# The order of two pairs of branch arms, with prefetch hints for the jumps over the arms not taken

## The chip, the core and the metric

The kernel runs on one core of a Trainium2 chip. A core has five engines that run side by side, each with its own stream of instructions and its own sequencer: TensorE (PE, matmuls; its weight loads are shown as PEld), VectorE (DVE), ScalarE (ACT), GpSimd (POOL) and SyncE (SP, which here only issues transfers). They meet through semaphores. Data moves between the chip's memory and the on-chip buffer by DMA, and so does code: the instructions lie in memory and are fetched in blocks.

The metric is the device time of one execution, in microseconds, as the median of several runs. A branch is taken by each engine for itself: all five load the flag into a register and jump or fall through, each at its own time.

## What is computed

One layer of a Perceiver-like network in float32, for 256 tokens of width 512: attention with 16 heads over 4096 context positions and the tokens themselves, then a state-space block (Mamba-2), then a mixture of 32 experts of which each token uses 6, with a shared expert beside them. Each part adds to the residual stream. Cut to what matters here:

```python
x = x + attention(layernorm(x), ctx, wq, wk, wv, wo, wk_ctx, wv_ctx, q_norm_w, k_norm_w)
x = x + mamba2(layernorm(x), W_in, conv_w, conv_b, dt_bias, A_log, D, norm_weight, W_out)

h = layernorm(x)
scores = sigmoid(h @ gate_w)
topk_w, topk_i = top_k(scores, 6)
topk_w = topk_w / (sum(topk_w) + 1e-20)
routed = sum over the 6 experts e of topk_w[e] * ((silu(h @ wg[e]) * (h @ wu[e])) @ wd[e])
shared = (silu(h @ sg) * (h @ su)) @ sd
return x + routed + shared
```

## The kernel before

The tokens stand in two tiles of 128 (`NT = 2`, `x_sb[:, t, :]`). Ahead of everything (L85 to L110) small constants are made, SP issues the first loads (the first piece of the context, `wk_ctx` in three pieces, `x`, the rest of the context's first piece, `wv_ctx`), and DVE works out a flag `small_scores` from the norm weights: whether attention scores are bounded so that the softmax needs no running maximum.

**The outer branch** (L1601, L1602). `values_load` lets every engine load the flag. The whole layer is then written twice, once as `layer(lctx, True)` (bounded scores) and once as `layer(lctx, False)` (the general case). In this program the arms lie in memory in the order in which the code has them: bounded, general, closing. With the inputs used here the flag is 1 and the bounded arm runs. Its first work on PE is the projection of the first context piece to keys (`ps_k`, L220), which waits for that piece and for `wk_ctx`.

**The inner branch** (L1558, L1572). The experts are computed in `NP = 16` rounds of two experts. The rounds have room for a certain number of tokens per expert; an expert with more is "crowded", and `crowded` says whether there is one. The value is loaded into `some` on every engine (L1558, in the middle of the rounds; each engine reaches the load where the order built for it puts it). At the end, if `some == 0`, the cheap arm runs: `finish(t)` adds the last sums, which PE has accumulated in `total[t]`, to `x_sb`, and `store(t)` sends the tile to the output, tile by tile. Otherwise the crowded arm computes all experts once more in full, and only then stores. With these inputs the cheap arm runs. In memory it lies between the rounds and the crowded arm, and behind that lies the whole general arm (on PE alone 3,823 instructions as the program is written, ahead of their expansion, and its own two inner arms), and then the closing code at L1651. So in the run shown every engine falls through both tests and then, at the end of the cheap arm, jumps over the crowded and the general arm to the closing code; the jump is on record under L1572 too.

At the end of an arm each engine raises the semaphores by what the other arm would have added, so that both arms leave the same counts. GpSimd does that for the counts of its indirect transfers with one instruction, `INC_SWDGE_SEM`.

**The closing code** (L1651). SP waits for all transfers and engines (12 semaphore instructions), then every engine passes a barrier: a DRAIN, then a semaphore that POOL gathers from the other four and releases. POOL clears the semaphores, and a second barrier follows.

What sets the order around the change: the scheduler places instructions by their dependencies within each engine's stream, block by block between branches. The order on SP is what matters for stores: an instruction waiting there holds up those behind it.

## Time and profile before

| | us |
|---|---|
| median of 3 runs | 983.04 (982.28 to 983.1) |
| the profiled execution | 983.11 |
| its span, first to last instruction | 981.4 |
| granted TensorE clock, mean | 0.997 of full |

Where the span goes, by stretches (busy time of PE in each):

| stretch, us | what runs | PE busy, us |
|---|---|---|
| 0 to 12 | constants, first loads, first keys | 6.8 |
| 12 to 730 | attention | 718 |
| 730 to 840 | state-space block, routing | 105 |
| 840 to 960 | rounds of experts | 120 |
| 960 to 972.8 | last round, last sums | 12 |
| 972.8 to 981.4 | stores, jump, closing code | 0 |

The page gives busy time per engine, but leaves out branches, semaphores, register loads and DMA issues. Those are found by asking for one line of the kernel: each row then names the engine (a "q" behind it is the engine's sequencer: "POOLq"), the operation, how often it stands there, its duration in ns (least, median, most) and when the first and the last of them started. "PEldq" is PE's sequencer. COMPARE_BRANCH is the record of any branch, conditional or not.

### The profile page before, as it was taken

The numbers are of one execution on the slowest core, as the hardware profiler recorded it, in microseconds if no ns is written. First come the engines' busy times: TensorE is split into PE (matmuls) and PEld (weight loads), VectorE is DVE, ScalarE is ACT, GpSimd is POOL, SyncE is SP. The second block draws the span as 40 slices with busy tenths as digits, with TensorE's granted clock in tenths as the row PEclk, the third lists the DMA queues.
The fourth block names the chain that finished last, engine by engine and source line by source line (L and its number), as shares of the span: only waits on it lengthen the run. The fifth ranks groups of instructions, "written<-read, shape, count | busy, mean of one in ns | idle before, by whom it ended". The sixth has DMA issues, their size and how long they took to land.

```text
span 981.4 us, 8877 instructions
## 1 busy us (share of the span) xinstructions
PE 961.9 (98%) x2730; PEld 454.0 (46%) x2730; DVE 497.0 (51%) x1000; ACT 388.0 (40%) x854; POOL 204.5 (21%) x212
## 2 busy tenths in 40 slices
PE   7999999999999999999999999999999999999996
PEld 3444444444444444444444444444465655555432
DVE  4456554454454544544545445358587656622124
ACT  3645443443443434434434344353153642122221
POOL 4443001101100200200200110000014133545433
PEclk9999999999999999999999999999999999999998
DMA  9734142213304304304213121160036353899974
GB/s 325 232 75 124 50 118 86 54 34 116 86 11 139 86 1 150 76 11 150 54 33 79 72 65 30 57 171 1 0 140 218 132 184 135 305 367 350 379 300 124
DMA packets 131164, 125.65 MB, mean 128 GB/s; under 512 B 80065, under 2 KB 99298, under 8 KB 125858
## 3 DMA queue, kind: packets, MB, share of 16 engines
q1 hardware_dynamic: 119216, 77.96, 26.5%
q0 software_dynamic: 7984, 41.16, 11.3%
q10 hardware_dynamic: 3906, 5.85, 1.7%
q8 instruction: 24, 0.39, 0.2%
q14 instruction: 34, 0.28, 0.1%
HBM read 89.02 MB, written 35.93 MB: 127 GB/s over the span
## 4 chain that ended last, share of the span: by engine, by line
PE 95%; ACT 1%; DVE 1%; POOL 1%; issue 0%; DMA 0%; SPq 0%; DVEq 0%
PE oT L594 23%; PE scT L569 23%; PE ps_kv L366 17%; PE ps_egu L220 5%; PE ps_self L220 3%; PE ps_v L220 2%; PE ps_o L792 2%; PE ps_egu L1390 2%; PE ps_k L220 2%; PE ps_ye L1460 2%; PE ps_xbc L220 1%; PE ps_out L986 1%; PE ps_sgu L220 1%; PE xgTp L1371 1%; PE ps_ye L1463 1%; PE ps_ye L1413 1%
## 5 line engine op out<-in xcount | busy, mean ns | idle before, releaser
L585 DVE TENSOR_TENSOR lacc<-lacc,prT 128x512 f32<-128x512 f32 x256 | 182.9, 715 | 239.0 <-ACT prT L575 238.3
L575 ACT ACTIVATE prT<-scT,bq,rk 128x512 f32<-128x512 f32 x256 | 198.8, 777 | 254.1 <-PE scT L569 241.7
L569 PE MATMUL scT<-qT,kT 128*128 128x512 f32 x536 | 271.6, 593 | 0.0
L594 PE MATMUL oT<-prT,v 128*128 128x512 f32 x528 | 268.3, 592 | 0.0
L569 PEld LDWEIGHTS scT<-qT,kT 128*128 128x128 f32 x536 | 101.2, 190 | 124.6 <-issue 121.4
L594 PEld LDWEIGHTS oT<-prT,v 128*128 128x128 f32 x528 | 100.3, 190 | 125.7 <-issue 115.5
L198 POOL TENSOR_TENSOR rk<-pv,mhalf 128x4 f32<-128x4 f32 x32 | 32.3, 1010 | 369.3 <-DVE pv L197 369.3
L256 ACT ACTIVATE sq<-kraw 128x128 f32<-128x128 f32 x128 | 35.6, 278 | 45.2 <-DVE kraw L384 43.2
L366 PE MATMUL ps_kv<-wkv,fast 128*128 128x512 f32 x112 | 53.5, 592 | 0.0
L366 PE MATMUL ps_kv<-wkv,ctx 128*128 128x512 f32 x112 | 52.8, 592 | 0.0
L366 PE MATMUL ps_kv<-fast,fast 128*128 128x512 f32 x112 | 52.6, 592 | 0.0
L600 DVE TENSOR_TENSOR oacc<-oT,oacc 128x512 f32<-128x512 f32 x64 | 43.7, 683 | 0.0
L366 PEld LDWEIGHTS ps_kv<-fast,fast 128*128 128x128 f32 x112 | 21.3, 190 | 26.8 <-issue 21.8
L366 PEld LDWEIGHTS ps_kv<-wkv,fast 128*128 128x128 f32 x112 | 21.3, 190 | 26.8 <-issue 26.8
L366 PEld LDWEIGHTS ps_kv<-wkv,ctx 128*128 128x128 f32 x112 | 21.3, 190 | 26.8 <-issue 23.7
L360 POOL TENSOR_TENSOR fast<-ctx 128x512 f32<-128x512 f32 x7 | 9.3, 1335 | 113.1 <-PE ps_kv L366 94.2
L384 DVE TENSOR_TENSOR kraw<-ps_kv,fast 128x256 f32<-128x256 f32 x42 | 17.8, 424 | 28.2 <-PE ps_kv L366 28.2
L1443 DVE TENSOR_TENSOR hid<-si,ps_egu 128x128 f32<-128x128 f32 x18 | 5.2, 286 | 49.8 <-ACT si L1441 49.8
L792 PE MATMUL ps_o<-wo,qT 128*128 128x512 f32 x64 | 28.8, 592 | 0.0
L220 PE MATMUL ps_self<-wq,xT 128*128 128x512 f32 x64 | 28.1, 592 | 0.0
L605 DVE RECIPROCAL lacc<-ps_l 128x512 f32<-128x512 f32 x8 | 26.8, 3348 | 0.1
L366 PE MATMUL ps_kv<-fast,ctx 128*128 128x512 f32 x56 | 26.3, 592 | 0.0
(379 smaller groups left out, 1118.8 us busy)
## 6 DMA issues: line engine op xcount, KB each, us to landing
xg<-xn SPq DMA_DIRECT2D x6, 2560.0 KB, 9.3
ctx<-in_ctxT_dram SPq DMA_DIRECT2D x7, 1024.0 KB, 5.3
kd<-tr SPq DMA_DIRECT2D x112, 64.0 KB, 2.4
kT<-kd SPq DMA_DIRECT2D x28, 256.0 KB, 2.9
ye<-y_sb ACTq DMA_DIRECT2D x21, 256.0 KB, 8.2
wq<-in_wq_dram SPq DMA_DIRECT2D x4, 1024.0 KB, 14.7
wo<-in_wo_dram SPq DMA_DIRECT2D x4, 1024.0 KB, 7.4
w_in<-in_W_inT_dram SPq DMA_DIRECT2D x4, 1024.0 KB, 5.7
```

The source lines that it names most:

```text
L198: return G.tensor_tensor(dst, v[:, :n], mhalf[:, :n], ALU.pow)
L220: TE.matmul(ps, lhs(k), rhs_of(k), start=(k == 0), stop=(k == KD - 1))
L256: S.activation(sq[:, h, :], raw[:, h, :], AF.Square, accum_out=ss[:, h:h + 1])
L366: TE.matmul(ps, lhs(k), rhs(k), start=(start and k == 0), stop=(k == 1), skip_group_check=True)
L569: scored.append(TE.matmul(sc, kT[:, g, i * P:(i + 1) * P], qT[:, t, heads4(g), :].rearrange("p h q -> p (h q)"), start=True, stop=True).ins)
L575: S.activation(pr, sc, AF.Exp, bias=shift, scale=SCALE if r is None else r[:, i, g:g + 1])
L585: V.tensor_tensor(la, la, pr, ALU.add)
L594: TE.matmul(outs[g, t], v[:, i, g * HD:(g + 1) * HD], pr, start=(n == 0), stop=last)
L600: V.tensor_tensor(ov, outs.pop((g, t)), ov, ALU.add)
L605: V.reciprocal(rl, ps)
L792: TE.matmul(m["ps_o", t], aT[:, t, h, :], wo[j][:, h % 4, :], start=(h == 0), stop=(h == NH - 1))
L1390: TE.matmul(ps[self.half(i)], xT[:, k, self.half(i)], w[i][:, k, :], start=(k == 0), stop=(k == KD - 1))
```

## The change

The arms change places. The general arm comes first in the outer branch, so the test is turned round (`flag == 0`) and the bounded arm is reached by a jump. Of the inner branch only the crowded arm is left, `finish` moves ahead of it and `store` behind it: both sums are made first, then a jump leads over the crowded arm, then both stores are issued. The bounded arm is now the last code ahead of the closing code. Two calls mark places for a prefetch hint, on all five engines: `"general"` ahead of the load of the flag, `"crowded"` behind the rounds. Each becomes one instruction per engine that names its branch as likely taken. In the built program they are the first instructions of their blocks: the first ones of the kernel's body, and the first ones of the arm.

```diff
@@ -1557,6 +1557,7 @@
                     weights_back()
                     some = nc.values_load(crowded, min_val=0, max_val=1)
                 (main.turn_hidden if wide else main.turn_hidden_halves)(n)
+            tc.mark_branch_hint_location("crowded", "LikelyTaken", mybir.ALL_ENGINES)
 
             spread_last(NP - 2, [0])
             main.down_here(NP - 1)
@@ -1569,13 +1570,10 @@
             def store(t):
                 nc.sync.dma_start(out[t * P:(t + 1) * P, :], x_sb[:, t, :])
 
-            with tc.If(some == 0) as arms:
-                for t in range(NT):
-                    finish(t)
-                    store(t)
-            with arms.Else():
-                for t in range(NT):
-                    finish(t)
+            for t in range(NT):
+                finish(t)
+
+            with tc.If(some == 1, label="crowded"):
                 main.weights = {}
                 for n in range(NP):
                     main.weights[n] = (held[2 * (n % 2)], held[2 * (n % 2) + 1], rests[n % 2])
@@ -1596,15 +1594,17 @@
                 V.tensor_copy(row2, row2f)
                 for t in range(NT):
                     add(gather(ye2, row2, t, [(main.e4, "xg")] * TOPK), t)
-                    store(t)
-
+            for t in range(NT):
+                store(t)
+
+    tc.mark_branch_hint_location("general", "LikelyTaken", mybir.ALL_ENGINES)
     flag = nc.values_load(small_scores, min_val=0, max_val=1)
-    with tc.If(flag == 1) as arms:
+    with tc.If(flag == 0, label="general") as arms:
+        with ExitStack() as lctx:
+            layer(lctx, False)
+    with arms.Else():
         with ExitStack() as lctx:
             layer(lctx, True)
-    with arms.Else():
-        with ExitStack() as lctx:
-            layer(lctx, False)
```

In the bounded arm, the instructions of every engine stand in the same order as before, but for the hint at its head and, on DVE, the two sums ahead of the load of `crowded` instead of behind the test. The first store waits, as the second does, for DVE's semaphore after it has been raised for the skipped arm.

## The prediction

> **What bounds the kernel now.** I read four views: the page (busy shares, queues, chain), then the chain of waits at both ends, then the branch lines and the closing line one by one, since the change is about branches and the page does not count them as work.

> ```profile
> span 981.4 us, 8877 instructions
> PE 961.9 (98%) x2730; PEld 454.0 (46%) x2730; DVE 497.0 (51%) x1000; ACT 388.0 (40%) x854; POOL 204.5 (21%) x212
> ...
> q8 instruction: 24, 0.39, 0.2%
> q14 instruction: 34, 0.28, 0.1%
> ```

> TensorE (PE) is busy for 98% of the span, so only what lies before its first and after its last matmul can be won, and whatever starts PE later is paid in full. The last two rows are queues that carry instructions: code is fetched by DMA, 0.39 MB in 24 packets (16 KB each) on one queue, 0.28 MB in 34 packets (8 KB each, a few tiny) on the other.

> The chain of waits at the two ends (start us, length us, what):

> ```profile
> 1.26 3.85 DMA wkv<-in_wk_ctx_dram
> 5.10 0.14 issue
> 5.24 13.00 PE ps_k L220 x24
> ...
> 969.40 2.67 PE total L1430 x6
> 972.07 0.02 issue
> 972.10 0.69 DVE x_sb L1567
> ```

> PE starts when the first piece of wk_ctx has landed, at 5.1. Its last matmul ends at 972.1, the last sum at 972.8. The span ends at 981.4: **8.6 us in which no engine computes.** What fills them stands in the rows of L1572 (the inner branch and the jump behind its arm) and L1651 (the closing of the kernel); columns: duration ns min/median/max, first and last start.

> ```profile
> L1572 ACTq COMPARE_BRANCH  x2: 34/36/38, 969.8 to 970.1; - x2
> L1572 DVEq COMPARE_BRANCH  x2: 51/53/55, 969.9 to 972.1; - x2
> L1572 PEldq COMPARE_BRANCH  x2: 63/2064/4064, 970.5 to 972.3; - x2
> L1572 POOLq INC_SWDGE_SEM  x1: 1767/1767/1767, 969.6 to 969.6; - x1
> ...
> L1572 POOLq COMPARE_BRANCH  x1: 41/41/41, 971.4 to 971.4; - x1
> ...
> L1572 SPq COMPARE_BRANCH  x1: 38/38/38, 973.6 to 973.6; - x1
> ```
> ```profile
> L1651 SPq EVENT_SEMAPHORE  x12: 27/28/28, 976.9 to 977.7; - x12
> ...
> L1651 POOLq DRAIN  x3: 40/107/6594, 973.9 to 981.1; - x3
> L1651 SPq DRAIN  x3: 7/7/130, 977.7 to 980.8; - x3
> L1651 ACTq DRAIN  x2: 8/44/81, 972.6 to 980.8; - x2
> L1651 PEldq DRAIN  x2: 8/40/73, 976.4 to 980.9; - x2
> L1651 DVEq DRAIN  x2: 10/34/57, 976.4 to 980.8; - x2
> ```

> Each engine meets L1572 twice: the test (falls through in this kernel) and the jump over the arms that were not taken. After the jump nothing runs for long: ACT 970.1 to 972.6 (2.5 us), POOL 971.4 to 973.9 (2.5), SP 973.6 to 976.9 (3.3, a semaphore wait may be in it), PE 972.3 to 976.4 (4.1, the 4064 ns of its row), DVE 972.1 to 976.4 (4.3). In the window from 970 to 982, instruction packets show on both queues. So **a taken jump to far code costs 2.5 to 4.3 us here**, while the tests that fell through cost 34 to 98 ns. What ends last is POOL: its first DRAIN starts at 973.9, takes 6.594 us and ends at 980.5, 1.1 us after SP's (979.4 by the trace). From there 0.8 us of barriers lead to 981.4.

> **The change, part by part**, against the profiled execution: 983.1 us, of which 981.4 are span and 1.7 lie outside it; the median of the runs is 983.04, 0.1 less.

> *The jump behind the arms goes (end).* The cheap arm now stands last, so its end runs straight into the closing code. On POOL, INC_SWDGE_SEM still starts at 969.6 (it waits for the last gather) and lasts 1.77; DRAIN then follows at 971.4 instead of 973.9: 2.5 us less. If it keeps its 6.6 us it ends at 978.0. Next in line is SP, below. The other three reach their DRAIN by 973 and wait.

> *Sums ahead of the branch, stores behind it.* DVE does both sums, then loads `crowded` (0.33 us, row of L1558), tests (0.05), jumps, and raises its semaphore for the skipped arm. By the built order both stores now wait for that raise. Load and test run beside the second sum (0.69 us), so if the jump is cheap the stores issue at about 972.9 and 973.4; today 972.0 and 972.8. The row of L1570 gives 3.8 us from issue to landing: 977.2. Queued behind the stores on SP are only the closing waits, mostly done by then (12 take 0.8 us today), so 0.3 us more: SP is through at 977.5, still 0.5 ahead of POOL. Cost nothing, covered by POOL's DRAIN; without that cover the delay of 0.6 counts in full.

> *Jumps over the crowded arm.* Five taken jumps are new. SP makes its own at about 846, POOL at 965, ACT at 970, PE at 970.5, with nothing behind them for microseconds; even at 4.1 us PE is through by 974.6. DVE's alone is exposed, at 972.5, since stores wait for it.

> *Jumps over the general arm (start).* Today PE tests at 3.5 and waits for its load until 5.1, a slack of 1.6 us. SP tests at 5.5; the first thing it then loads, wk, is wanted at 22.7 and lands 13.7 us after its issue at 5.6, 3.4 us in hand. ACT and DVE wait for loads too (tables, x). So PE decides.

> *Hints.* One per engine as first instruction of the kernel, one as first instruction of the arm: the built order has the second there, 960 us ahead of its branch, not where the code places it. No row shows a hint. From both sides: if it works, a jump costs about what a test does, 0.1 us, and the start loses nothing on PE; if it does nothing, PE's jump costs the row's 4.1 us: 3.5 + 4.1 = 7.6 instead of 5.2, 2.4 us lost. I take the hint as working, as it executes at 0.8, 2.7 us ahead of the branch, more than ACT's or POOL's whole jump, when no load is yet moving; that is a choice. Its instruction takes its turn ahead of SP's first load (SP's small instructions: 0.03 to 0.1 us), and 16 KB of code for PE beside the first loads may hold one piece of wk_ctx up by as much as the fetch, up to 1 us. Between 0 and 1 us I take **0.3**, nearer the low end, as the fetch comes first.

> [...]

> **Sum:** -2.5 (POOL) + 0.3 (start) = -2.2: 983.1 - 2.2 = 980.9, less the 0.1 to the median: **980.8 us**.

> **Cases.** Under 0.2% (2 us here) a difference does not count as a change; so faster is below 981.1, slower above 985.0.

> 1. *As above*, 980.8: 980.5 to 981.5 by the start's 0 to 1, and 980.1 to 981.9 with half the spread of the runs shown (982.3 to 983.1) on either side: 0.40. For it: POOL's jump is plainly in its rows and its DRAIN follows directly.
> 2. *POOL's DRAIN gets shorter too*, as it might end with something else that also moves. Then SP closes: 977.5 at the latest, 975.7 if the stores land 1.8 us sooner without instruction packets beside them; with the 0.8 the span ends at 978.3 to 976.5, -3.1 to -4.9, and +0.3: 978.4 to 980.2, middle 979.4: 0.20. Against it: nothing names what the DRAIN waits for.
> 3. *Given back.* Either the DRAIN ends at 980.5 whatever happens before it, or the outer hint comes too late for PE (+2.4 against -2.5). 982.8 to 983.8: 0.23. Against the first: all gathers have landed by 969.4 and the count is raised at 971.3, which leaves nothing for it to wait on.
> 4. *The hints do nothing*: the new jumps are paid where somebody waits. Start +2.4. At the end DVE's jump at 972.5 costs 4.3: the stores issue at 976.9 and 977.3, land by 981.1, SP closes at 981.4 instead of POOL at 980.5: +0.9. 983.0 + 3.3 = 986.3. It decides from the point where PE's jump costs over 1.6 us, and DVE's over about 0.6. For it: [...]the early place of the second hint: 0.17.

> Faster: 0.28 of case 1 and all of case 2, 0.48. Same: 0.12 of case 1 and case 3, 0.35. Slower: case 4, 0.17. The range 978.6 to 985.3 leaves out most of case 4 and the fastest end of case 2. Case 1's own is 980.1 to 981.9.

> **What would show it.** L1576 in place of L1572: POOL's INC_SWDGE_SEM at 969.6 and DRAIN right behind it, with its length (6.6, or case 2 or 3). PE's first ps_k at 5.2 to 5.6 rather than 7.6. The stores at 972.9 and 973.4 rather than 977. No instruction packets from 970 on, and five early ones near 1 us. If PE's row of the outer branch shows about 4 us, the forecast is wrong at the hint; if POOL's DRAIN still ends at 980.5, it is wrong at the DRAIN.

## The result, and the profile after

| | before | after |
|---|---|---|
| median of the runs, us | 983.28 (8 runs, 982.28 to 985.02) | 985.72 (8 runs, 985.35 to 988.44) |
| the profiled execution, us | 983.11 | 985.35 |
| its span, us | 981.4 | 983.6 |
| first ps_k product starts, us | 5.2 | 9.4 |
| last sum ends, us | 972.8 | 977.8 |
| last sum to the span's end, us | 8.6 | 5.8 |

The ratio of the times is 1.003, 95% interval 1.0021 to 1.004: **slower by 0.3%**, where 980.8 us were forecast. The end gave about what was forecast (2.8 us, for 2.5), and the start lost 5.0.

The page of the kernel after, and its chain of waits at both ends (start us, length us, what):

```profile
span 983.6 us, 8882 instructions
PE 962.8 (98%) x2730; PEld 454.0 (46%) x2730; DVE 499.8 (51%) x1000; ACT 388.0 (39%) x854; POOL 204.8 (21%) x212
...
q8 instruction: 25, 0.41, 0.2%
q14 instruction: 34, 0.28, 0.1%
```
```profile
1.35 3.72 DMA wkv<-in_wk_ctx_dram
5.07 4.32 issue
9.38 13.61 PE ps_k L220 x24
...
977.09 0.02 issue
977.11 0.69 DVE x_sb L1568
```

The work is the same: 2730 matmuls, and PE busy for 0.9 us more. The first data are there at 5.07 as before, but between data and first product stand 4.32 us of "issue" in place of 0.14: PE waited for nothing that is data. One more 16 KB packet of code came in on q8. The branch rows of the outer test say where PE stood (duration ns min/median/max, first and last start us). First PE's row in the kernel before, then all engines in the kernel after, then the hints:

```profile
L1602 PEldq COMPARE_BRANCH  x1: 98/98/98, 3.5 to 3.5; - x1
```
```profile
L1602 ACTq COMPARE_BRANCH  x1: 68/68/68, 3.6 to 3.6; - x1
L1602 POOLq COMPARE_BRANCH  x1: 64/64/64, 3.7 to 3.7; - x1
L1602 PEldq COMPARE_BRANCH  x1: 5424/5424/5424, 3.7 to 3.7; - x1
L1602 DVEq COMPARE_BRANCH  x1: 78/78/78, 3.7 to 3.7; - x1
L1602 SPq COMPARE_BRANCH  x1: 70/70/70, 5.8 to 5.8; - x1
```
```profile
L1651 ACTq BRANCH_PREFETCH_HINT  x2: 35/48/60, 0.8 to 9.8; - x2
...
L1651 PEldq BRANCH_PREFETCH_HINT  x2: 31/40/50, 0.9 to 9.2; - x2
```

PE's record holds the whole stand at the jump, 5.4 us. The other engines' records end at once; how long they stood is read from the next instruction, which is the second hint: ACT tests at 3.6 and goes on at 9.8. So every engine stood for 5.1 to 6.3 us here, although its hint had run at 0.8 to 0.9. By the trace no packet of code starts before 6.75 (PE's), 3.05 us *after* PE's branch. It ends at 7.8, and PE goes on at 9.1, 1.3 us later. In every jump of these runs for which PE had to wait for code it goes on 1.3 to 1.8 us after its packet has ended, so it is the packet that it stands for. In the old jump the packet started 1.7 us after the branch. In the stretch from 5 to 9 us the 16 DMA engines are full with the first loads (share 1.02 to 1.07); in the old jump's stretch, 970 to 976, the share was 0.01 to 0.56.

The end, by the rows of the inner branch and of the closing code:

```profile
L1576 POOLq INC_SWDGE_SEM  x1: 1780/1780/1780, 974.4 to 974.4; - x1
L1576 ACTq COMPARE_BRANCH  x1: 54/54/54, 974.8 to 974.8; - x1
...
L1576 PEldq COMPARE_BRANCH  x1: 359/359/359, 975.5 to 975.5; - x1
...
L1576 DVEq COMPARE_BRANCH  x1: 68/68/68, 977.5 to 977.5; - x1
```
```profile
L1651 POOLq DRAIN  x3: 40/109/6525, 976.3 to 983.4; - x3
L1651 SPq DRAIN  x3: 7/7/7, 981.3 to 983.1; - x3
```

POOL's DRAIN now starts right behind INC_SWDGE_SEM (974.4 + 1.8), before the last sum ends; before it stood 2.6 us behind it. It takes 6.5 us as before and still closes the span. PE's jump over the crowded arm is 0.36 us where the jump of before was 4.1.

### The profile page after: what moved, and what is told of

The parts are those of the page before. It is cut to its first block, busy times and chain, and to the rows that moved or that the text cites. A ratio compares the mean times of both kernels' runs of the same rounds, so it can differ in the third digit from the quotient of the medians.

```text
span 983.6 us, 8882 instructions
## 1 busy us (share of the span) xinstructions
PE 962.8 (98%) x2730; PEld 454.0 (46%) x2730; DVE 499.8 (51%) x1000; ACT 388.0 (39%) x854; POOL 204.8 (21%) x212
## 3 DMA queue, kind: packets, MB, share of 16 engines
q0 software_dynamic: 7984, 41.16, 11.4%
## 4 chain that ended last, share of the span: by engine, by line
PE 95%; ACT 1%; DVE 1%; issue 1%; POOL 1%; DMA 0%; SPq 0%; DVEq 0%
PE scT L569 23%; PE oT L594 23%; PE ps_kv L366 17%; PE ps_egu L220 5%; PE ps_self L220 3%; PE ps_v L220 2%; PE ps_o L792 2%; PE ps_egu L1390 2%; PE ps_k L220 2%; PE ps_ye L1460 2%; PE ps_xbc L220 1%; PE ps_out L986 1%; PE ps_sgu L220 1%; PE xgTp L1371 1%; PE ps_ye L1463 1%
## 5 line engine op out<-in xcount | busy, mean ns | idle before, releaser
L220 PE MATMUL ps_self<-wq,xT 128*128 128x512 f32 x64 | 28.1, 592 | 0.0
L220 PE MATMUL ps_k<-wkv,ctx 128*128 128x512 f32 x32 | 17.2, 700 | 9.4 <-issue 9.4
```

What stands on the lines that cost most here:

```text
L220: TE.matmul(ps, lhs(k), rhs_of(k), start=(k == 0), stop=(k == KD - 1))
```

## The experiments

The question was which part does what, and why one hint worked and the other did not. My theory at first, called **block theory** below: code is read in blocks (in the kernel before, PE's 16 KB packets come once per some 250 records of its stream), and a hint is acted on only if its branch stands in a block that is entered after the hint has run. The inner hint has 960 us and many blocks between it and its branch; the outer one has, on PE, only the load of the flag. The rivals: the lead of 2.7 us is too short (**lead theory**), or the loss has another cause. Below, "jump" is the time from the branch to the next instruction that the engine meets behind it.

### One part at a time

The outer edit undone (`e1_inner_only`), the inner edit undone (`e2_outer_only`), each hint taken out (`e3_no_outer_hint`, `e4_no_inner_hint`):

```diff
# e1: outer branch as before
-    with tc.If(flag == 0, label="general") as arms:
+    with tc.If(flag == 1) as arms:
# e2: inner branch as before
-            with tc.If(some == 1, label="crowded"):
+            with tc.If(some == 0) as arms:
# e3
-    tc.mark_branch_hint_location("general", "LikelyTaken", mybir.ALL_ENGINES)
# e4
-            tc.mark_branch_hint_location("crowded", "LikelyTaken", mybir.ALL_ENGINES)
```

> The inner branch as in the changed kernel, the outer branch in the old order: its bounded arm comes first again and there is no outer hint. Block theory (a hint is acted on only where an engine's program comes to the branch in a stretch of code that it had not yet read when the hint ran; the inner hint qualifies, the outer doesn't): the start is that of the kernel before, PE's first ps_k product at 5.1 to 5.4 us. At the end every engine that leaves the bounded arm now jumps over the general one without a hint, as before, but the inner jump stays short, stores go out near 973.5 us, and POOL's DRAIN, which starts when POOL has jumped, closes the span as it did before: 982 to 983.5 us of time. Rival, the loss isn't from the start's jump: the first ps_k product is early and yet the time stays at 985 or more.

> The outer branch as in the changed kernel (general arm first, with its hint), the inner one as before (each arm has its own sums and stores, the short arm first, no hint). Block theory: the start loses the same 5 us as in the changed kernel, first ps_k product at 9.4 us; at the end the stores go out of the short arm at once, then a jump over the crowded arm without a hint, of 2.5 to 4.3 us on each engine, stands where before the jump over the general arm stood, so nothing is won there: 987.5 to 989 us. Rival, the loss comes with the inner edit and not the outer: near 983 us, the first ps_k product at 5.2 us.

> The changed kernel without the outer hint; the arms stay in their new order. Block theory: the outer hint did nothing, so the time is that of the changed kernel, 985.0 to 986.2 us, the first ps_k product at 9.2 to 9.6 us, jumps of 5 to 6 us on every engine. Rival, the hint works in part (it shortens the fetch, or fetches the wrong piece and so delays it): the jump of PE changes by 1 us or more and the time with it, to 987 or more if the hint helped and to 984 or less if it harmed.

> The changed kernel without the inner hint; sums and stores are placed as in the changed kernel. If the inner hint is what makes the end short: every engine jumps over the crowded arm for 2.5 to 4.3 us. SP reaches the branch early (its jump lies under the last products) and the stores wait for the sums alone, or for DVE's jump if the code order holds them; POOL's DRAIN starts 2.5 us later, as POOL jumps only when the last weights are read. With POOL's DRAIN closing, the span ends 2 to 3 us later than in the changed kernel: 987.5 to 989 us. Rival, the hint is worth nothing (the jump lies beside other work): 985.3 to 986.2 us.

| | median us | ratio to before, 95% | first ps_k | last sum to end |
|---|---|---|---|---|
| inner edit alone | 983.32 | 1.0, 0.9991 to 1.0009 | 5.1 | 10.1 |
| outer edit alone | 985.72 | 1.0026, 1.0018 to 1.0033 | 10.6 | 5.2 |
| after, no outer hint | 985.43 | 1.0024, 1.0017 to 1.0031 | 9.9 | 5.9 |
| after, no inner hint | 986.35 | 1.0031, 1.0019 to 1.0042 | 10.3 | 6.9 |

(The last two columns are single profiles. That of the inner edit alone ran 2.4 us above its median, so its 10.1 is not a price.) **The whole change of the time comes with the outer edit, both its loss at the start and its gain at the end; the outer hint is worth nothing.** PE's outer branch with the outer edit alone, and in the changed kernel without the outer hint:

```profile
L1603 PEldq COMPARE_BRANCH  x1: 6882/6882/6882, 3.6 to 3.6; - x1
```
```profile
L1601 PEldq COMPARE_BRANCH  x1: 6165/6165/6165, 3.5 to 3.5; - x1
```

My expectation for the outer edit alone, 987.5 or more, was wrong: I had put a price on POOL's jump over the crowded arm alone, which is 0.16 us there. So what POOL paid for in the kernel before (2.6 us) was the general arm. Without the inner hint the rows show what it does:

```profile
L1575 PEldq COMPARE_BRANCH  x1: 3651/3651/3651, 975.1 to 975.1; - x1
...
L1575 DVEq COMPARE_BRANCH  x1: 71/71/71, 977.1 to 977.1; - x1
...
L1575 DVEq EVENT_SEMAPHORE  x1: 21/21/21, 980.2 to 980.2; - x1
```

DVE jumps for 3.1 us (977.1 to 980.2; with the hint 0.6), the stores wait for it and issue at 980.2 and 980.7, and SP closes at 983.4 instead of POOL at 982.5. That is 1 us of tail in the profile, where I had expected 2 to 3; in the medians, 986.35 against 985.43 and 985.72, it is not resolved.

### Does the outer hint need lead or distance?

`e5_filler` puts instructions between hint and branch, `e6_late_flag` puts time there and hardly any instruction:

```diff
# e5, ahead of the load of the flag
+        ...
+        for i in range(300):
+            G.memset(fill[:, i:i + 1], 0.0)
+        for i in range(80):
+            TE.matmul(fill_ps[:, i:i + 1], ident, ones[:, 0:1], start=True, stop=True)
# e6, ahead of the flag's first operation
+        ...
+        V.memset(big, 0.0)
+        for _ in range(5):
+            V.tensor_scalar(big, big, 0.5, None, ALU.mult)
+        V.tensor_tensor(nb[:, 0:1], nb[:, 0:1], big[0:1, 0:1], ALU.add)
```

> The changed kernel with instructions that compute nothing for the result put between the outer hint and the outer branch: 300 one-column memsets on POOL and 80 one-column products on PE, so that on these two engines the branch comes to lie in code that is read only after the hint has run; ACT, DVE and SP get nothing. Their time is added to the start, so only the jumps are read. Block theory: on POOL and PE the jump is short (0.3 to 1 us from the branch to the next instruction) and on ACT, DVE and SP it is still 5 to 6.5 us. Lead theory (the hint needs more than the 2.7 us that it has in the changed kernel): the filler delays the branch on PE and POOL by more than 10 us and would make it short there as well, so this run alone tells only that a hint at the start can work; the run with the late flag tells the two apart. Rival, a hint is lost while the program's first loads fill the DMA engines: POOL's and PE's jump stays at 4 to 6 us.

> The changed kernel with a chain of seven VectorE operations that delays the flag by some 12 us; nothing else is added, so on PE, ACT, POOL and SP the hint and the branch keep their places in the code and the hint's lead grows from 2.7 to some 14 us. Its time grows by the delay, so only the jumps are read. Lead theory (2.7 us were too few): the jump is short (under 1 us) on PE, ACT, POOL and SP. Block theory (the branch stands in code that was read before the hint ran): the jump is still 2.5 us or more on every engine, nearer 2.5 to 4.5 if the first loads have thinned out by then.

The branch rows with the filler, then with the late flag:

```profile
L1609 POOLq COMPARE_BRANCH  x1: 70/70/70, 12.2 to 12.2; - x1
L1609 PEldq COMPARE_BRANCH  x1: 387/387/387, 32.6 to 32.6; - x1
```
```profile
L1608 PEldq COMPARE_BRANCH  x1: 4181/4181/4181, 10.6 to 10.6; - x1
```

With the filler PE goes on after 0.4 us and POOL after 0.5; ACT, DVE and SP, which have none, jump for 5.0 to 5.8. With the late flag PE's lead is 9.7 us (the delay came out at 7 us, not 12), and the jump is 4.2 us on PE and 4.0 to 4.9 on the others; PE's fetch starts at 12.3, 1.7 us after the branch. **Lead is not it:** POOL's 9.8 us there bring no early fetch (jump 4.9 us), where 11.4 us with 300 more instructions between give 0.5.

An alignment directive moves the branch to the next multiple of 256 instructions without adding work, over padding that is jumped (that a block begins there was my assumption; the traces show some 250 records between PE's packets, not where a block begins): `w4_aligned` on all engines, `w5_aligned_nohint` the same without the hint, `w6_pe_aligned` on PE alone.

```diff
+    for e in (TE, V, S, G, nc.sync):
+        e.addr_align(256, max_nops=0)
     flag = nc.values_load(small_scores, min_val=0, max_val=1)
```

> The changed kernel with one alignment directive per engine between the outer hint and the load of the flag: it moves the flag's load and the outer branch to the start of the next block[...], over padding that is jumped and not executed. No work and no lead time is added. Block theory (a hint is acted on only if its branch lies in a block that is entered after the hint ran): the jump over the general arm becomes short on every engine (0.2 to 1 us instead of 5 to 6), the first ps_k product starts at 5 to 6 us as in the kernel before, the tail after the last sum stays 5.8 us, and the time is 980.3 to 981.8 us, faster than both kernels. Lead theory: 2.7 us of lead are still too few, the jump stays 4 to 6 us and the time 985 to 986.5 us. A cost that either may see: the jump over the padding itself, if the next block is not there yet (2 to 3 us).

> The same with the alignment directives and without the outer hint. If hint and block together make the jump short, as the block theory says: jumps of 4 to 6 us on every engine, first ps_k product at 9.2 us or later, 985 to 986.5 us. Rival, the alignment alone shortens the jump (its target is in the piece that is fetched next anyway): the same times as with the hint.

> The changed kernel with the alignment directive on PE alone. With the directives on all engines PE's own jump over the padding took 0.35 us, its fetch ran at 2.1 us and the hinted jump 0.5 us; what was lost there was the flag, because VectorE's jump over padding held it to 6.5 us. So with PE alone: flag at 3.1 us as in the changed kernel, PE's jump under 1 us, first ps_k product at 4.5 to 5.8 us; ACT, DVE, POOL and SP still jump for 5 to 6.5 us, as in the changed kernel, and come out at about 10 us. Block theory and PE as the bound at the start: tail 5.8 us as in the changed kernel, 980.3 to 982.0 us, faster than both kernels. Rival, the late ACT and DVE hold PE after its first two ps_k tiles: PE starts at 5.2 but the sums' end comes 2 us or more later than in the kernel before, 983 us or more.

PE's outer branch on all-engine alignment:

```profile
L1604 PEldq COMPARE_BRANCH  x1: 462/462/462, 7.1 to 7.1; - x1
```

Without the hint the same jump took 6.6 us. So on PE hint and distance together make it short. On the other four, whose branches the directive moved as well, my expectation of 0.2 to 1 us failed: they jump for 3.3 to 4.3 us (without the hint SP for 3.6 and the others for 7.2 to 7.3), and their packets come behind the branch. So the same move is not enough there. The time was not won: 985.49 us (ratio 1.0025, 1.0019 to 1.0032), without the hint 989.9. The cost that I had named in passing decided: the jump over the padding was short on PE (0.35 us); behind DVE's, its first operation for the flag came at 5.7 us instead of 2.3, so that PE could load the flag at 6.5 instead of 3.1. With the directive on PE alone the flag comes at 3.7, PE jumps for 1.6 us, and the time is 982.67 us, ratio 0.9997 (0.9989 to 1.0005): level with before, 0.7 us above what I expected at most. (Its profiled execution ran 3.3 us above that median.) The first ps_k product started at 6.8, not at 5.8 or earlier, since the first data came later; the reason is shown below. ACT, DVE and POOL came out of their jumps after 2.6 to 3.6 us, not after 5 or more as I had expected.

### How much distance

`e7_short_filler` has 8 products on PE and 32 memsets on POOL in place of 80 and 300; `w8_pe_filler` the 8 products alone, `w9_pe_filler_nohint` those without the hint, `e8_two_products` two products with it:

```diff
+        for i in range(8):
+            TE.matmul(fill_ps[:, i:i + 1], ident, ones[:, 0:1], start=True, stop=True)
     tc.mark_branch_hint_location("general", "LikelyTaken", mybir.ALL_ENGINES)
```

In the built program the hint still stands first, the products behind it.

> The long filler cut down to 8 one-column products on PE (32 records of its array and weight loads) and 32 one-column memsets on POOL between the outer hint and the outer branch, so that the branch stands some 35 instructions behind the hint but, by the count of records between PE's fetches, still in the same block[...]. Block theory: as in the changed kernel, PE's fetch comes after its branch (at 3.5 to 4.5 us) and PE's jump takes 4 to 6.5 us, POOL's 5 to 7 us. Rival, a distance of some tens of instructions is enough (which the run with two key tiles ahead hints at, where PE's fetch came 3 us before its branch): a fetch on PE's queue ahead of its branch or less than 1 us after it, and PE's jump under 3 us.

> The changed kernel with 8 one-column products on PE between the outer hint and the outer branch, and nothing added on the other engines. If some tens of instructions between hint and branch suffice on PE (distance theory): PE's fetch at about 2 us, its jump at most 2.5 us, first ps_k product at 6 to 7 us, because the early fetch runs beside the first loads (in the run with the short filler SP's issue of them stood for 3.0 us), tail 5.9 us, and the time 981.5 to 983 us, at or just under the kernel before. Block theory: fetch after the branch, jump 5 to 6.5 us, 985 to 986.5 us.

> The same without the outer hint. If it is the hint that starts PE's early fetch: fetch 2 to 4 us after the branch, jump 5 to 6.5 us, SP's first issues without a stop, 985 to 986.5 us. Rival, the products on PE start the fetch[...] and the hint adds nothing: the same times as with the hint.

> The filler cut to 2 one-column products, 8 records on PE between hint and branch in place of 32. Distance theory with a bound above some ten instructions: as in the changed kernel, fetch after the branch at 3.6 us, jump 5 to 6.5 us. With a bound below: fetch at 2 us and a jump under 2.5 us, as with 8 products.

PE's outer branch with 8 products and the hint, with 8 products without the hint, with two products and the hint:

```profile
L1606 PEldq COMPARE_BRANCH  x1: 2202/2202/2202, 3.6 to 3.6; - x1
```
```profile
L1605 PEldq COMPARE_BRANCH  x1: 5726/5726/5726, 3.5 to 3.5; - x1
```
```profile
L1606 PEldq COMPARE_BRANCH  x1: 5441/5441/5441, 3.6 to 3.6; - x1
```

PE's fetch starts at 2.04 in the first (and in `e7_short_filler`), ahead of the branch, and at 6.28 in the second and 6.66 in the third. The queues of the first, with the window from 0 to 6 us, in which the other two and the kernel after have no packet of code at all:

```profile
q8 instruction: 1, 0.02, 2.5%
q14 instruction: 3, 0.02, 1.7%
```

It does not follow that a hint starts a fetch at once. The fetch at 2.04 comes 1.1 us after the hint, but 0.4 us after the products could start (1.64). In `e5_filler` PE's packet starts at 20.2, 19 us after the hint and still ahead of the branch. The inner hint, which runs at 9.2 on PE, shows no packet of its own: PE's last one ahead of the inner branch starts at 964.3 with it and at 964.0 without (`e4_no_inner_hint`), and only without it PE then stands for one more, from 976.1. So the hint seems to change what a later fetch brings. That is a reading; and as the hint is the first instruction everywhere, these runs don't tell the distance from it from the branch's place in the code.

With 8 products the time is 986.72 against 988.70 us for the kernel before in the same comparison (that chip was slower throughout): ratio **0.9985, 0.9977 to 0.9994**, a little faster than before, and faster than after. Without the hint the ratio is 1.0011 (1.0004 to 1.0018). That is less loss than without the hint and without the products (1.0024); the two intervals only touch, and I have no cause for it.

The chain of the kernel with 8 products shows the rest of the start's price:

```profile
1.35 0.43 SPq L95
1.78 0.04 issue
1.82 2.94 SPq L95
```

SP issues the first loads one after the other in 0.4 us each; here one issue takes 2.94 us, and the next starts behind it at 4.81, while PE's 16 KB packet is on the way (2.04, for 2.36 us). In the kernel after it took 0.43, and the packet, at 6.75, 1.03. PE goes on 1.4 us after the packet's end, so the 2.2 us left of its jump are the slow packet, and the first product starts at 6.8 instead of 5.2, when its data are there. That the packet causes the stop is inferred from the five runs that have both (a packet for PE near 2 us and an issue of 2.4 to 3.0 us) and from its absence where PE's fetch is late. While the issue stands, the DMA engines are freer (share 0.29 from 4 to 5 us, in the kernel after 0.93), and the packets of ACT, DVE and POOL start at 4.5 to 4.8 us instead of 7.4 to 7.6: their jumps take 3.1 to 3.3 us there.

### Ways round the start that did not pay

`w2a_two_branches`: the bounded arm first, then the general arm as a branch of its own, so that nothing is jumped at the start and the hint has 960 us; `w2b_two_branches_inner` with the inner edit as well, `w2c_two_branches_nohint` without the hint.

```diff
-    with tc.If(flag == 1) as arms:
-        ... layer(lctx, True)
-    with arms.Else():
-        ... layer(lctx, False)
+    tc.mark_branch_hint_location("general", "LikelyTaken", mybir.ALL_ENGINES)
+    with tc.If(flag == 1):
+        ... layer(lctx, True)
+    with tc.If(flag == 0, label="general"):
+        ... layer(lctx, False)
```

> The inner branch as before; the outer one taken apart into two branches that follow each other: first the bounded arm if the flag is 1, then the general arm if it is 0, with a hint ahead of both for the jump over the general arm. At the start nothing is jumped over, and the only jump over the general arm is at the end, 960 us after its hint. If a hint is acted on where its branch lies in code that is read after it (block theory), or where it has a long lead (lead theory), the jump at the end is short on every engine (under 1 us in place of the 2.5 to 4.3 us of before) and the start is that of before: first ps_k product near 5.1 us, sums' end near 972.8, POOL's DRAIN from about 972 for 6.5 us, span 978.8 to 979.6, time 980 to 981.3 us, faster than both kernels. Rival, a hint so far ahead is lost, or the inner branch's gain came from elsewhere: jumps as before and 983 to 984 us.

> As the run with two branches, but with the inner branch as in the changed kernel[...]. If an engine keeps both: start as before, the tail after the last sum 5.8 to 6.2 us as in the changed kernel, 980.3 to 981.8 us. If the second hint displaces the first: the end's jump over the general arm is 2.5 to 4.4 us again and the time is that of the run with the inner edit alone, 982.8 to 984 us.

> The two branches that follow each other without the hint, inner branch as before. If the hint makes the difference: the jump at the end is 2.5 to 4.3 us on PE, DVE and POOL as in the kernel before, 982.5 to 984 us. Rival, taking the branch apart makes the difference, not the hint: 980 to 981.3 us.

983.62, 985.41 and 985.81 us; ratios 1.0003 (0.9995 to 1.0011), 1.0034 (1.0021 to 1.0047) and 1.0036 (1.0023 to 1.005). I was wrong on all three: the first came 2.3 us above its range (and into its rival's), the other two 1.4 and 1.8 above the highest that I had given. The rows of the first at the second branch:

```profile
L1606 POOLq INC_SWDGE_SEM  x1: 1737/1737/1737, 973.8 to 973.8; - x1
L1606 PEldq COMPARE_BRANCH  x1: 4047/4047/4047, 977.0 to 977.0; - x1
```

The hint worked on POOL alone (jump 0.5 us; without the hint 2.7). The other four stand there for 2.6 to 4.3 us, PE for 4.1; they come to this branch through an unhinted far jump over the crowded arm (on POOL that one takes 0.3), which I take for the cause. And the second branch brings POOL a second INC_SWDGE_SEM of 1.7 us, ahead of its DRAIN in all three runs, which takes most of POOL's gain. With two hints out at once (the second of the three) the jump over the general arm is 2.6 to 4.1 us on every engine, on POOL 2.9 in place of 0.5. That the later hint, or the jump that it served, has undone the earlier is a reading of this one run.

`w1_keys_ahead`: two ps_k tiles and two small loads put ahead of the branch, with one pair of PSUM banks shared by both arms.

> The changed kernel with the first two ps_k tiles (8 products on PE) and the two small loads on ACT's queue issued ahead of the outer branch, so that PE's array has some 6 us of work while its sequencer waits at the jump. If the whole loss is PE's wait at the start: the products run from 5.2 to about 11.5 us, PE's jump of 5 to 6 us lies beside them for the most part, and of the 5 us at the start 2 to 4.5 come back: 981 to 983.5 us. Rival, the other engines' jumps (ACT and DVE come out at 9.8 to 10 us) hold PE as much as its own: nothing is won, 985 to 986 us.

1003.99 us, ratio 1.0207. The shared banks changed the schedule far behind the start (PE busy 63.7 of the 70 us from 30 to 100, in the kernel after 70.0), so the time says nothing on the start. Its start alone can be read: PE's jump was 0.5 us, and its fetch began at 10.1, ahead of the branch at 13.2. That agrees with the distance (32 records of products in between). The fetch came 9 us after the hint; until 6.0 PE waited for its first data, and a later wait for data ended at 9.7, 0.4 us ahead of the fetch. Why it came then is open.

## Why the prediction was wrong, point by point

- **"I take the hint as working"**: this step failed. The start was put at +0.3 and cost +5.0 by the last sum. The hint ran at 0.8 to 0.9, as forecast, with the lead of 2.7 us that I counted on, and nothing was fetched ahead of the branch: the run without it is the same. I argued from time and from free DMA engines; on PE the hint needs distance in the code. The early packets "near 1 us" that I had named as the sign did not come. What happened is the second half of case 3 (no help from the outer hint, POOL's gain kept), at more than its price. The chances were too small: no row of the profile spoke for that hint, and its place right ahead of its branch was in the built order.
- **The price if it fails, +2.4**, was mis-sized as well. It took PE's jump at 4.1 us from the end of the kernel, where the DMA engines' share was 0.56 at most; at the start it was 5.5, as the packet came 3.05 us after the branch and not 1.7. Why it came later is not settled. The first loads are the likely cause, but with the late flag, at a DMA share of 1.03 to 1.06, it came after 1.7 again. First product 9.4 instead of 7.6: +4.1 in place of +2.4 (or of the 0.3 taken). To that come 0.6 in the first 24 products (13.61 against 13.00; PE starts with products of 1.06 us before they become 0.59, here two more of them) and some 0.3 later: +5.0 at the last sum.
- **POOL's DRAIN 2.5 us earlier, same length**: right. Counted from the last sum, the DRAIN starts 1.5 us before its end instead of 1.2 after it, and the tail is 2.8 shorter. In all profiles taken its length is 6.5 to 6.6 us, whatever lies before it, so the second case (a shorter DRAIN) falls and so does the half of the third in which its end is fixed. +5.0 - 2.8 = +2.2, and the two profiled executions differ by 2.24.
- **Stores and sums covered by POOL**: right. The stores issue 0.35 and 0.8 us after the last sum, land in 2.5 (I had taken 3.8), and SP is through at 981.3, 1.4 us before POOL. The inner hint, 960 us ahead, works on PE, ACT and DVE (0.4 to 0.6 us, without it 2.5 to 3.7), and without it SP closes. On POOL, which goes on after 0.7 us either way, and on SP, which waits behind its branch, nothing can be read.
- **Case 4, hints that do nothing, 986.3**: the nearest of the four to the 985.7 measured; my chance of 0.17 for it was an estimate. It came near by luck: its end of +0.9 was 3.7 us too high, as the inner hint works and POOL's gain stayed, and its start of +2.4 was 2.6 too low. That the jump is paid in full at the start was right (5.5 us on PE); that a hint is worth nothing was not, as the inner hint (PE's jump 0.36 us, without it 3.65) and the run with 8 products (2.2 us, without the hint 5.7) show.

## What to carry to other kernels

A taken jump over the general arm cost every engine 2.5 to 4.3 us at the end of the kernel before and 5.1 to 6.3 us at the start of the kernel after; the kernel after's jump over the crowded arm, without its hint, 2.5 to 3.7 us on PE, ACT and DVE and 0.7 us on POOL. Put such a jump where no engine is waited for, and not on the way to the first matmul. Count on a prefetch hint only where a run shows its jump to be short. At the start, 8 records between hint and branch were too few on PE and 32 enough, 32 memsets too few on POOL and 300 enough; the sign on PE was a packet of code ahead of the branch (2.04 us against 3.6). At the end, with another hint in between, the jump took 2.6 to 4.1 us on every engine, and with an unhinted far jump in between 2.6 to 4.3 us on all but POOL (0.5). A price read at the quiet end of a kernel need not be the price at its start (PE: 4.1 us and 5.5 us).

## What the runs showed of the hardware that I had not expected

- The far jump: 2.5 to 4.3 us at the end of the kernel before, 5.1 to 6.3 us at the start of the kernel after.
- With 8 PE records between hint and branch PE's fetch comes behind the branch (6.66 us), with 32 ahead of it (2.04 us, 10.1 in `w1_keys_ahead`); 9.7 us of lead without them did not bring it ahead of the branch (12.3 us, branch at 10.6).
- PE goes on 1.3 to 1.8 us after the end of the packet that it waits for, in all runs with such a jump.
- With a second hint for another branch behind it, POOL's jump at the first one's branch took 2.9 us in place of 0.5 (one run).
- An early 16 KB fetch beside the first loads took 2.4 us instead of 1.0 (8 products), and with it one issue on SP stood for 2.9 us instead of 0.4.
